# Block aggregates multiplied together with h, seven products for eight throughout, in a two-layer graph network

## The chip, the cores and the metric

The kernel runs on one core of one Trainium2 chip, in fp32. The metric is the device time of one launch in microseconds (us), the median of three runs. The profile is one profiled execution of the same program: its durations are exact for that execution, and its span (first to last instruction) is what the durations add up to.

## The reference

There are 64 graphs of 256 nodes and 512 features. Every graph passes through two layers. Both take `h = relu(layernorm(x))` and add their result to `x`. Cut to what matters:

```python
def layer0(x, adj, W):                      # W is 512 x 1024, [W1 | W2]
    h = relu(layernorm(x))
    T = adj / max(rowsum(adj), 1e-6)
    return x + relu(h @ W1.T + (T @ h) @ W2.T)

def layer1(X, A, Wv, bv, aw, ab, Wk, bk):   # Wk is 3 x 512 x 512
    h = relu(layernorm(X))
    Xw = h @ Wv + bv
    sj, si = Xw @ aw[:d, 0], Xw @ aw[d:, 0]
    e = leaky_relu(sj[:, None, :] + si[:, :, None] + ab, 0.2)
    a = A * exp(e)
    T = a / (rowsum(a) + 1e-12)
    return X + relu(h @ Wk[0] + T @ h @ Wk[1] + T @ T @ h @ Wk[2] + bk[0] + bk[1] + bk[2])
```

`T` is 256 x 256 for each graph. The scores need no 512 x 512 product, since `h @ Wv @ aw` is `h` times a vector that is worked out once.

## The kernel before

**Tiles.** 256 nodes are NC = 2 blocks of 128 partitions, 512 features are FC = 4 blocks. A product `h @ B` is cut into 2 x 2 blocks and computed as seven block products in place of eight (`seven`, L242; a Strassen form). `blocks` (L229) makes the four sums of blocks of the turned `h` on GpSimd; the sums of blocks of the weights are made once at the start (`combine`, L90). Each of the seven products is two matmuls, over two blocks of 128 of the features, into one of three PSUM banks, and ScalarE and VectorE move intermediate sums between them (L252 to L275).

**Turning.** TensorE wants its left operand with the summed index on the partitions, so `h`, adj and `T` are turned. `Flip` (L205) turns 32 x 32 squares on VectorE (L215), stores the four stripes to DRAM (L220) and loads them back in the turned order (L225). The first and last graphs are turned on TensorE (`flipped_on_pe`, L113).

**Layer 0** (`layer0`, L321): `seven` multiplies h by [W1 | W2] at once: 14 matmuls of 512 columns. Then `spread` (L278) adds `T (h W2)` in four ordinary matmuls of 512, and VectorE adds relu of the result to x (L332).

**Layer 1** is four pieces. `own` (L350) is `h Wk[0]` with the two score vectors as two extra columns per half: 14 matmuls of 258 columns. `transition` (L363) sends sj through DRAM to get it as a row on all partitions (ds, row), and makes T: exponentials on ScalarE (L377), maximum and products on VectorE (L380, L384), scaling (L393), turning. `pair` (L405) is `h [Wk[1] | Wk[2]]`: 14 matmuls of 512. `twice` (L410) adds `T q` (four matmuls of 512), copies `u` out (L425), and adds `T u` (four more); VectorE finishes and SP stores (L433, L435).

**Order.** Each piece is a generator that yields between steps, and strings of letters say which piece takes its next step: FIRST for the beginning, TURN for every graph from 4 on, LAST for the end. In one TURN the kernel works on layer 0 of graph g, own of g-1, pair and transition of g-2 and twice of g-3. Instructions stay in the order in which they are written, on each engine by itself. All DMAs are issued by SP.

The PSUM banks are three for layer 0 (bank0), three for layer 1 (bank1) and two that own shares with bank0 (bank2).

Of the kernel before, what the change touches and what calls it, by code (L numbers as in the profile page):

```python
# [15 lines left out]
P = 128  # L16
Q = 32
# [4 lines left out]


def bcast(ap, offset, n):

    return bass.AP(tensor=ap.tensor, offset=ap.offset + offset, ap=[[0, P], [1, n]])
# [3 lines left out]
def gnn_two_layers(ctx: ExitStack, tc: tile.TileContext, x, adj, w0, wv, bv, aw, ab, wk, bk, out):  # L30

# [7 lines left out]
    const = ctx.enter_context(tc.tile_pool(name="const", bufs=1))  # L56
    loads = ctx.enter_context(tc.tile_pool(name="loads", bufs=3))
    early = ctx.enter_context(tc.tile_pool(name="early", bufs=2))
    small = ctx.enter_context(tc.tile_pool(name="small", bufs=4))
    work = ctx.enter_context(tc.tile_pool(name="work", bufs=1))  # L60
    psum = ctx.enter_context(tc.tile_pool(name="psum", bufs=1, space=bass.MemoryType.PSUM))
    banks0 = [psum.tile([P, F], FP, name=f"bank0_{i}") for i in range(3)]
    banks1 = [psum.tile([P, F], FP, name=f"bank1_{i}") for i in range(3)]
    banks2 = [psum.tile([P, F], FP, name=f"bank2_{i}") for i in range(2)]
    dram = ctx.enter_context(tc.tile_pool(name="dram", bufs=2, space=bass.MemoryType.DRAM))

    X, A = {}, {}

    def load(g, what):
        if what is X:  # L70
            X[g] = loads.tile([P, NC, F], FP, name="x")
            nc.sync.dma_start(X[g], x[g].rearrange("(c p) f -> p c f", p=P))
        else:
            A[g] = loads.tile([P, NC, N], FP, name="a", bufs=4)
            nc.sync.dma_start(A[g], adj[g].rearrange("(c p) j -> p c j", p=P))

    names = ("b11", "b21", "b22", "t1", "t2", "t3", "t4")

    def forms(name, width):

        return {k: const.tile([P, FC // 2, width], FP, name=f"{name}_{k}") for k in names}

    B0, B1, B2 = forms("l0", F), forms("l1", F), forms("l1s", HW)
    bk_sb = const.tile([P, F], FP, name="bk_sb")
    c0 = const.tile([P, 1], FP, name="c0")
    ident = const.tile([P, P], FP, name="ident")
    mhalf = const.tile([P, NC], FP, name="mhalf")
    zero = const.tile([P, F], BF, name="zero")

    def combine(b, b12, eng=(nc.vector,) * 4):  # L90

        for e, to, x, y in zip(eng, ("t3", "t1", "t2", "t4"), ("b22", None, "b22", "b21"), (None, "b11", "t1", "t2")):
            e.tensor_sub(b[to], b12 if x is None else b[x], b12 if y is None else b[y])  # L93
            yield

    def turned_on_pe(blocks, banks):

        for i in range(0, len(blocks), FC):
            pt = next(banks).rearrange("p (k n) -> p k n", k=FC)
            for k, block in enumerate(blocks[i : i + FC]):  # L100
                nc.tensor.transpose(pt[:, k, :], block, ident)  # L101
            yield pt

    def weights_l0(w0_sb, b12, banks):

        for side, to in enumerate(((B0["b11"], B0["b21"]), (b12, B0["b22"]))):
            pts = turned_on_pe([w0_sb[oc][:, (side * FC + k) * P :][:, :P] for oc in range(FC) for k in range(FC)], banks)
            for oc, pt in enumerate(pts):
                for kh in range(2):
                    (nc.scalar.copy if oc % 2 else nc.vector.tensor_copy)(to[kh][:, :, oc * P : (oc + 1) * P],  # L110
                                                                         pt[:, 2 * kh : 2 * kh + 2, :])

    def flipped_on_pe(src, width, banks, pool, name, bufs=1):  # L113

        t = pool.tile([P, width // P, P, NC], FP, name=name, bufs=bufs)
        for c in range(NC):
            for pt in turned_on_pe([src[:, c, k * P : (k + 1) * P] for k in range(width // P)], banks):
                (nc.scalar.copy if c else nc.vector.tensor_copy)(t[:, :, :, c], pt[:, : width // P, :])
        return t

    def spare(name, bufs=1):

        return work.tile([P, 2, F], FP, name=name, bufs=bufs).rearrange("p s f -> p (s f)")

    def weights_l1():


        aw_sb = spare("x1", 4).rearrange("p (s f) -> p s f", s=2)
        wv_sb = [work.tile([P, NC, 2, HW], FP, name="e", bufs=2).rearrange("p c s w -> p (c s w)")[:, : 2 * F]
                 .rearrange("p (c f) -> p c f", c=2) for _ in range(2)]  # L130
        b12s = spare("u")[:, : FC // 2 * HW].rearrange("p (c w) -> p c w", w=HW)
        b12 = spare("o").rearrange("p (c f) -> p c f", f=F)
        scr, bv_sb = (work.tile([P, F], FP, name=n) for n in ("z0", "z1"))
        two = work.tile([P, FC, P, NC], FP, name="h1t", bufs=2).rearrange("p k n c -> p (k n c)")
        biases = [two[:, :F], two[:, F:], work.tile([P, F], FP, name="tt")]
        vc = small.tile([P, 2, FC], FP, name="vc", bufs=1)
        cc = small.tile([P, 2], FP, name="cc", bufs=1)
        ab_sb = small.tile([P, 1], FP, name="ab_sb", bufs=1)
        src = [wk[k].rearrange("(h c p) o -> h p c o", p=P, h=2) for k in range(NW)]
        nc.sync.dma_start(aw_sb, bcast(aw, 0, 2 * F))  # L140
        for h in range(2):
            nc.sync.dma_start(wv_sb[h], wv.rearrange("(h c p) o -> h p c o", p=P, h=2)[h])
        halves = ((b12s, 0, 1), (B2["b22"], 1, 1), (B2["b11"], 0, 0), (B2["b21"], 1, 0))
        for to, kh, col in halves:
            nc.sync.dma_start(to[:, :, :half], src[0][kh][:, :, col * half : (col + 1) * half])
            nc.gpsimd.memset(to[:, :, half + 1], 0.0)
        yield
        for to, k, kh in ((b12, 2, 0), (B1["b22"], 2, 1), (B1["b11"], 1, 0), (B1["b21"], 1, 1)):
            nc.sync.dma_start(to, src[k][kh])
        nc.sync.dma_start(bv_sb, bcast(bv, 0, F))  # L150
        nc.sync.dma_start(ab_sb, bcast(ab, 0, 1))
        for k in range(NW):
            nc.sync.dma_start(biases[k], bcast(bk, k * F, F))
        yield
        sums = combine(B1, b12, (nc.gpsimd,) * 4)
        for c in range(FC):
            next(sums)
            for s in range(2):
                nc.vector.scalar_tensor_tensor(scr, wv_sb[c // 2][:, c % 2, :], 1.0, aw_sb[:, s, :], op0=ALU.mult,  # L159
                                               op1=ALU.mult, accum_out=vc[:, s, c : c + 1])  # L160
            yield
        for to, kh, col in halves:
            nc.vector.tensor_copy(to[:, :, half], vc[:, col, 2 * kh : 2 * kh + 2])
        yield from combine(B2, b12s)
        for s in range(2):
            nc.vector.scalar_tensor_tensor(scr, bv_sb, 1.0, aw_sb[:, s, :], op0=ALU.mult, op1=ALU.mult,
                                           accum_out=cc[:, s : s + 1])
        nc.vector.scalar_tensor_tensor(c0, cc[:, 0:1], cc[:, 1:2], ab_sb, op0=ALU.add, op1=ALU.add)
        nc.vector.tensor_add(bk_sb, biases[0], biases[1])
        nc.vector.tensor_add(bk_sb, bk_sb, biases[2])  # L170
        yield


    def finished(steps):

        while True:
            try:
                next(steps)
            except StopIteration as end:
                return end.value  # L180

    def norm_relu(src):

        stats = small.tile([P, NC, 6], FP, name="stats")
        mv = small.tile([P, NC, 2], FP, name="mv")
        for c in range(NC):
            nc.vector.bn_stats(stats[:, c, :], src[:, c, :])  # L187
            nc.vector.bn_aggr(mv[:, c, :], stats[:, c, :])  # L188
            if c == 0:
                yield  # L190
        ve = small.tile([P, NC], FP, name="ve")
        nc.gpsimd.tensor_scalar(ve, mv[:, :, 1], LN_EPS, None, op0=ALU.add)  # L192
        rstd = small.tile([P, NC], FP, name="rstd")
        nc.gpsimd.tensor_tensor(rstd, ve, mhalf, op=ALU.pow)  # L194
        yield
        nmr = small.tile([P, NC], FP, name="nmr")
        nc.vector.scalar_tensor_tensor(nmr, mv[:, :, 0], -1.0, rstd, op0=ALU.mult, op1=ALU.mult)  # L197
        h = early.tile([P, NC, F], FP, name="h", bufs=1)
        for c in range(NC):
            nc.scalar.activation(h[:, c, :], src[:, c, :], AF.Relu, bias=nmr[:, c : c + 1],  # L200
                                 scale=rstd[:, c : c + 1])
            yield
# [345 lines left out]
```

## Time and profile before

| what | us |
|---|---|
| median of three runs (2642.81 to 2645.36) | 2644.55 |
| span of the profiled execution | 2643.6 |
| TensorE busy, share of the span | 2612.3, 99% |
| VectorE busy | 1204.4, 46% |
| ScalarE busy | 897.2, 34% |
| GpSimd busy | 524.2, 20% |
| granted TensorE clock, mean | 0.997 |

The profile lists, for each engine, groups of like instructions: source line, engine, operation, names of what is written and read, shape and count, then the busy time, the mean of one in ns, and the idle time ahead of them with what ended it. PE is TensorE, PEld its weight loads, DVE VectorE, ACT ScalarE, POOL GpSimd, SP the engine that issues DMAs. Matmul durations hold the time until the last result has left the array; the next matmul starts earlier, so the distance from start to start is the cost of one. An fp32 matmul appears as two records. In the timeline a line has start, length, engine, line, operation, names, shape and count. The chain of waits is followed back from the last instruction: each piece was released by the one before it.

### The profile page before, as it was taken

To read this page: it belongs to the slowest core of one execution; us is meant where nothing else is said; L and a number is where in the kernel's file an instruction comes from. 1 tells how busy PE (TensorE), PEld (TensorE's weight loads), DVE (VectorE), ACT (ScalarE), POOL (GpSimd) and SP (SyncE) were. 2 spreads that over 40 slices of the span, in tenths; PEclk is the share of its full clock that TensorE was granted. 3 is DMA by queue.
4 is the path that set the end of the run, shared out by engine and by line. 5 is a ranking of instruction groups with operands and counts; after the bars stand their busy time and mean duration, and the time that the engine had idled before them with its cause. 6 is when DMAs were issued, how large, how long until landed. Compare 5 with 4: busy or idle time off the path is not lost.

```text
span 2643.6 us, 23486 instructions
## 1 busy us (share of the span) xinstructions
PE 2612.3 (99%) x6983; PEld 1347.6 (51%) x6983; DVE 1204.4 (46%) x2664; ACT 897.2 (34%) x1807; POOL 524.2 (20%) x785
## 2 busy tenths in 40 slices
PE   7999999999999999999999999999999999999999
PEld 3544555555545545555555455555555554555554
DVE  5544444444444444444444444444444444444433
ACT  2333333333333333333333333333333333333332
POOL 3311211221121112111211221121112112211210
PEclk9999999999999999999999999999999999999999
DMA  5444454454454444444444445444445454454421
GB/s 183 108 126 119 108 118 110 111 123 106 120 120 100 121 115 112 116 111 112 123 103 123 116 103 122 113 112 116 111 114 123 100 125 116 104 122 109 110 74 44
DMA packets 576222, 298.93 MB, mean 113 GB/s; under 512 B 418784, under 2 KB 540640, under 8 KB 576096
## 3 DMA queue, kind: packets, MB, share of 16 engines
q1 hardware_dynamic: 576096, 297.44, 46.3%
q8 instruction: 56, 0.92, 0.1%
q14 instruction: 70, 0.57, 0.1%
HBM read 165.15 MB, written 132.19 MB: 112 GB/s over the span
## 4 chain that ended last, share of the span: by engine, by line
PE 97%; DVE 1%; issue 0%; ACT 0%; DMA 0%; SPq 0%; POOL 0%; DVEq 0%; ACTq 0%
PE bank L240 97%; PE bank L101 0%; DVE z L159 0%; DVE l_t L93 0%; DMA x<-in_x_dram 0%; DMA row<-ds 0%; DVE turned L215 0%; SPq L220 0%; DVE stats L187 0%; ACT z L377 0%; DVE nmr L197 0%; DVE o L433 0%; ACT an L296 0%; DVE l1s_t L93 0%; POOL rstd L194 0%
## 5 line engine op out<-in xcount | busy, mean ns | idle before, releaser
L240 PE MATMUL bank<-l_t,h1t_s 128*128 128x512 f32 x780 | 367.4, 594 | 0.7 <-ACT bank L252 0.7
L240 PE MATMUL bank<-l_t,h0t_s 128*128 128x512 f32 x756 | 356.9, 595 | 4.1 <-DVE l_t L93 3.4
L252 ACT COPY bank<-bank 128x512 f32<-128x512 f32 (+1 forms) x192 | 95.9, 499 | 710.7 <-PE bank L240 710.7
L215 DVE STREAM_TRANSPOSE turned<-h 128x512 f32<-128x512 f32 x252 | 178.4, 709 | 298.0 <-ACT h L200 298.0
L233 POOL TENSOR_TENSOR h0t_s<-h0t 128x256 f32<-128x256 f32 x63 | 53.3, 847 | 982.9 <-DMA h0t<-dh0t 880.3
L240 PE MATMUL bank<-l_b,h1t 128*128 128x512 f32 x520 | 244.4, 592 | 0.1
L240 PE MATMUL bank<-u,tt 128*128 128x512 f32 x512 | 242.1, 596 | 2.3 <-ACT u L425 2.3
L240 PE MATMUL bank<-q,tt 128*128 128x512 f32 x512 | 240.0, 592 | 1.3 <-DMA tt<-dtt 1.3
L240 PE MATMUL bank<-q,ant 128*128 128x512 f32 x512 | 232.5, 596 | 5.3 <-DVE q L275 5.3
L240 PEld LDWEIGHTS bank<-l_t,h0t_s 128*128 128x128 f32 x756 | 143.8, 191 | 183.5 <-issue 169.1
L240 PE MATMUL bank<-l_b,h0t 128*128 128x512 f32 x504 | 237.2, 593 | 0.0
L192 POOL TENSOR_SCALAR ve<-mv 128x2 f32<-128x2 f32 x128 | 29.2, 228 | 1020.4 <-DVE mv L188 1011.8
L200 ACT ACTIVATE h<-x,nmr,rstd 128x512 f32<-128x512 f32 x256 | 202.2, 818 | 17.7 <-DVE nmr L197 17.7
L240 PEld LDWEIGHTS bank<-l_t,h1t_s 128*128 128x128 f32 x780 | 147.7, 190 | 109.7 <-issue 97.0
L240 PEld LDWEIGHTS bank<-l1s_t,h1t_s 128*128 128x128 f32 x768 | 146.5, 191 | 102.7 <-issue 84.1
L240 PE MATMUL bank<-l1s_t,h1t_s 128*128 128x258 f32 x768 | 198.7, 381 | 0.0
L268 DVE TENSOR_TENSOR q<-bank,m 128x512 f32<-128x512 f32 x128 | 88.5, 692 | 202.2 <-PE bank L240 201.2
L332 DVE SCALAR_TENSOR_TENSOR x<-bank,x 128x512 f32<-128x512 f32 x128 | 88.5, 692 | 197.7 <-PE bank L240 197.7
L187 DVE BATCH_NORM_STATS2 stats<-x 128x6 f32<-128x512 f32 x256 | 172.2, 673 | 5.0 <-DMA x<-in_x_dram 5.0
L240 PEld LDWEIGHTS bank<-q,ant 128*128 128x128 f32 x512 | 100.8, 197 | 124.3 <-issue 109.4
L240 PEld LDWEIGHTS bank<-u,tt 128*128 128x128 f32 x512 | 100.6, 197 | 121.5 <-issue 88.4
L240 PEld LDWEIGHTS bank<-q,tt 128*128 128x128 f32 x512 | 100.5, 196 | 120.8 <-issue 116.3
(109 smaller groups left out, 3250.7 us busy)
## 6 DMA issues: line engine op xcount, KB each, us to landing
x<-in_x_dram SPq DMA_DIRECT2D x64, 512.0 KB, 5.6
dh1t<-turned SPq DMA_DIRECT2D x256, 128.0 KB, 2.8
h1t<-dh1t SPq DMA_DIRECT2D x64, 512.0 KB, 3.9
out_dram<-o SPq DMA_DIRECT2D x64, 512.0 KB, 3.2
dh0t<-turned SPq DMA_DIRECT2D x248, 128.0 KB, 2.9
h0t<-dh0t SPq DMA_DIRECT2D x62, 512.0 KB, 4.2
a<-in_adj_dram SPq DMA_DIRECT2D x64, 256.0 KB, 3.2
dant<-turned SPq DMA_DIRECT2D x248, 64.0 KB, 1.9
```

The lines of the kernel that those rows point to most:

```text
L187: nc.vector.bn_stats(stats[:, c, :], src[:, c, :])
L192: nc.gpsimd.tensor_scalar(ve, mv[:, :, 1], LN_EPS, None, op0=ALU.add)
L200: nc.scalar.activation(h[:, c, :], src[:, c, :], AF.Relu, bias=nmr[:, c : c + 1], scale=rstd[:, c : c + 1])
L215: nc.vector.transpose(self.turned.rearrange("p b r c -> p c b r")[:, c], src.rearrange("p c (b s) -> p c b s", s=Q)[:, c])
L233: nc.gpsimd.tensor_add(s1, a21, a22)
L240: nc.tensor.matmul(ps, lhs, rhs, start=start, stop=stop, skip_group_check=True)
L252: nc.scalar.copy(r, p)
L268: nc.vector.tensor_add(c22, p, m167)
L332: nc.vector.scalar_tensor_tensor(x1[:, c, :], banks[1 + c], 0.0, x[:, c, :], op0=ALU.max, op1=ALU.add)
```

## The change

The kernel is rewritten around three ideas.

1. Aggregation comes first. Layer 0 computes `z = T h` and then `[h | z] @ [W1 ; W2]` as one block product with the long inner dimension: each of the seven products sums over h and z in one bank before it is decoded (`main`). Layer 1 computes `z = T h`, `q = z Wk[2]`, and then `h Wk[0] + z Wk[1] + T q`, again as seven products over all three terms (`outer`). `T T h Wk[2]` is thus `T (z Wk[2])`, and the aggregate stays in its encoded form: `spread` writes the four blocks of z and the three sums of them that the next product wants as left operands.
2. Every product is a seven-product form, those with T too. `left_of_t` makes the four sums of blocks of T, `right_of_h` those of h, both on GpSimd. `spread` takes h as the stationary operand and T as the moving one, 128 columns wide, so that z comes out turned. The scores are four products with accumulation on VectorE of h with two vectors `v = Wv @ aw`, made at the start and spread through DRAM.
3. The order is data. `Plan.add` records each instruction with what it reads and writes; `emit` sorts each engine's instructions by a number from a table (AT), one per instruction of a stage, plus graph x TURN, plus a shift for the first and last five graphs (SHIFT).

In the steady turn TensorE works on aggregate and layer0 of graph g, `once` (layer 1's z) and `inner` (q) of g-1, and `outer` of g-2. One DMA per piece and the ways of turning stay as they were.

```diff
+EDGE = 5
+TURN = 41.62
+AT = {
+    "aggregate": (-3.8, 0.1, -3.6, 5.6, -18.4, -16.1, 2.2, -2.0, 2.2, 3.7, 9.3, 4.8, 4.4, 4.5, 5.0, 5.2, 14.3, 6.9, 13.8, 12.7, 10.0, 17.0, 11.4,
+        18.9, 21.4),
...
+class Plan:
+    def stage(self, name, graph=None, shift=None):
+        self.name, self.graph, self.count = name, graph, 0
+        self.base = 0.0 if graph is None else graph * self.turn + self.shift.get((name, shift), 0.0)
+    def emit(self):
+        queues = {}
+        for i in sorted(range(len(self.ops)), key=lambda i: self.ops[i][3]):
+            queues.setdefault(self.ops[i][0], []).append(i)
...
+    def left_of_t(tt, s):
+        (t, tk), (sv, sk) = tt, s
+        a11, a12, a21, a22 = (t[:, k, :, c] for c in range(2) for k in range(2))
+        tks, ks = [tk, tk + "'"], parts(sk, 4)
+        pool_op("tensor_add", 0.55, sv[:, 0], a21, a22, tks, ks[0])
+        pool_op("tensor_sub", 0.55, sv[:, 1], sv[:, 0], a11, tks + ks[:1], ks[1])
+        pool_op("tensor_sub", 0.5, sv[:, 2], a11, a21, tks, ks[2])
+        pool_op("tensor_sub", 0.5, sv[:, 3], a12, sv[:, 1], tks + ks[1:2], ks[3])
...
+    def spread(left, right, out, banks):
+        (z, zk), (m, mk), (bx, by) = out, MZ[0], banks
+        def turned(k, b, cols, start=False):
+            (l, lk), (r, rk) = left[k], right[k]
+            def run():
+                for i in range(2):
+                    at = cols.start + i * P
+                    matmul(bank[b][:, at : at + P], r[:, i * P : (i + 1) * P], l, start and i == 0)
+            add("PE", 0.001684 * half, run, lk + rk, [f"bank{b}"])
+        turned(1, by, lo, True)
+        turned(5, bx, lo, True)
+        copy(*m1, by, lo)
+        minus(*m15, *m1, bx, lo)
+        turned(2, by, lo)
+        turned(6, by, hi)
+        turned(4, bx, lo)
+        turned(7, bx, hi)
+        copy(*zf(0), by, lo)
+        plus(*u, by, hi, *m15)
+        copy(*zf(3), bx, lo)
+        plus(*zf(2), bx, hi, *u)
+        turned(3, by, hi)
+        plus(*zf(1), by, hi, *m15)
+        pool_op("tensor_sub", 0.85, z[:, 4], z[:, 3], z[:, 0], at(3)[1] + at(0)[1], f"{zk}.4")
+        pool_op("tensor_add", 0.85, z[:, 5], z[:, 4], z[:, 2], at(4)[1] + at(2)[1], f"{zk}.5")
+        pool_op("tensor_add", 0.85, z[:, 6], z[:, 4], z[:, 1], at(4)[1] + at(1)[1], f"{zk}.6")
...
+    def main(terms, banks, bias):
+        p, r, d = banks
+        step(5, p, lo, terms, True)
+        if bias:
+            l5, k5 = lo5, "lo5"
+            minus(l5[:, 1], ["lo5.1"], bk_hi, ["bk"], p, lo)
+        else:
+            copy(m5_0, ["m5_0"], p, lo)
+        step(1, p, lo, terms, True)
...
+        step(6, p, lo, terms)
...
+        step(7, p, lo, terms)
...
+        step(2, r, lo, terms)
+        step(3, r, hi, terms)
+        step(4, d, lo, terms)
...
+    def turn1(g):
+        norm_relu(g, of(X, g), next(norms), (h, hk))
+        for s in range(2):
+            for c in range(NC):
+                add("DVE", 0.85, lambda s=s, c=c: nc.vector.scalar_tensor_tensor(scr.rearrange("p c n -> p (c n)"), h[:, c, :], 1.0, v_sb[:, s, :],
+                                                                               op0=ALU.mult, op1=ALU.mult, accum_out=sj[:, s, c : c + 1]),
+                    [f"{hk}.{c}", "v"], parts(sck) + [f"{sjk}.{s}{c}"], port=True)
...
+    def once(g):
+        zs[g] = spread(lefts[g], right_of_h(rights1.pop(g), HF[1]), ZG[0], (6, 7))
+    def inner(g):
+        step(1, by, lo, terms, True)
+        step(7, bx, lo, terms, True)
+        copy(*m1, by, lo)
+        plus(*m17, bx, lo, *m1)
+        step(2, by, lo, terms)
+        step(6, by, hi, terms)
+        step(3, bx, lo, terms)
+        step(4, bx, hi, terms)
+        copy(*b11, by, lo)
+        plus(*u3, by, hi, *m17)
+        copy(*t3, bx, lo)
+        plus(*t2, bx, lo, *b11)
+        plus(*b21, bx, hi, *u3)
+        step(5, by, hi, terms)
+        plus(*b22, by, hi, *m17)
+        pool_op("tensor_sub", 0.85, nt1[0], t2[0], b22[0], t2[1] + b22[1], nt1[1][0])
+        pool_op("tensor_sub", 0.85, t4[0], b21[0], t2[0], b21[1] + t2[1], t4[1][0])
+    def outer(g):
+        banks = (3, 4, 5)
+        main([(left_of_h(H1T[0], S1[0]), weights(W1F, "l1", 0)), (zs.pop(g), weights(W1F, "l1", 1)), (lefts.pop(g), qs.pop(g))], banks, True)
+        finish(g, banks)
...
+    ORDER = ("aggregate", "prepare", "layer0", "prepared", "turn1", "loads", "moved", "once", "inner", "turned1", "outer", "transition")
-    TURN = "EU NL NEU mUIL NL NNU NEL ENU EUL ENL ENL EP NL L IO MP MO MP O MP EMO NMP O P O O MOP"
```

In the turn of the changed kernel the names are: `s0` and `s1` the sums of blocks of the turned h for layer 0 and 1 (the text also says s00 and s10 for their buffers), `hf0` and `hf1` those of h as right operand, `sa` and `st` those of T, `ag` and `zg` the seven forms of z, `qf` those of q, `ant` and `tt` the turned T, banks 0 to 2 layer 0, 3 to 5 outer, 6 and 7 the spreads and inner. `step(k)` is one of the seven products over all its terms.

## The prediction

> **What bounds the kernel now.** I read the page's first part (busy time of each engine), then its chain of waits, then the timeline of TensorE over one round of the loop.
>
> ```profile
> PE 2612.3 (99%) x6983; PEld 1347.6 (51%) x6983; DVE 1204.4 (46%) x2664; ACT 897.2 (34%) x1807; POOL 524.2 (20%) x785
> ...
> 149.00 2448.84 PE bank L240 x6540
> ...
> 1300.21 1.88 PE L240 MATMUL bank<-u,tt 128*128 128x512 f32 x4
> 1301.93 1.88 PE L240 MATMUL bank<-l_t,h0t_s 128*128 128x512 f32 x4
> ...
> 1315.66 1.03 PE L240 MATMUL bank<-l1s_b,h1t 128*128 128x258 f32 x4
> 1316.54 1.88 PE L240 MATMUL bank<-l_t,h1t_s 128*128 128x512 f32 x4
> ...
> 1340.65 1.88 PE L240 MATMUL bank<-u,tt 128*128 128x512 f32 x4
> ...
> 2603.14 0.60 PE L101 MATMUL bank<-ident,an 128*128 128x128 f32 x4
> 2603.58 1.88 PE L240 MATMUL bank<-l_t,h1t_s 128*128 128x512 f32 x4
> ```
>
> TensorE is the bound, and it does not wait: from 149.00 to 2597.84 us the chain is one piece of L240. So the time is TensorE's instructions times their spacing, and everything on the other engines is cover. The starts give the spacing. Every fp32 matmul is two records ("passes"). Four of 512 columns take 1301.93 - 1300.21 = 1.72 us, 0.429 each; four of 258 take 0.88, 0.218 each; four transposes of 128 columns, each with a weight load of its own, 0.44, 0.110 each. That is a straight line: two cycles of 2.4 GHz per column and some 2.5 ns. The mean durations of the groups (594 and 381 ns) hold the drain and aren't the spacing.
>
> Check on a whole turn: 40 matmuls of 512 and 14 of 258 are 80 x 0.429 + 28 x 0.2177 = 40.42 us. The timeline has u,tt at 1300.21 and again at 1340.65: 40.44. So 64 turns are 2587, and 56 of the span's 2643.6 us are filling and draining (for 0 to 149 and 2597 to the end TensorE's work is spread thin). The median of the runs, 2644.55, lies 1 us above the span; I add that at the end.
>
> The helpers' prices come from the groups by line and shape, and the DMA issues (last number: us to landing):
>
> ```profile
> L187 DVE BATCH_NORM_STATS2 stats<-x 128x6 f32<-128x512 f32 x256 | 172.2, 673 | 5.0 <-DMA x<-in_x_dram 5.0
> L268 DVE TENSOR_TENSOR e<-bank,m_s 128x258 f32<-128x258 f32 x64 | 27.3, 426 | 14.4 <-PE bank L240 14.4
> L159 DVE SCALAR_TENSOR_TENSOR z<-e,x 128x512 f32<-128x512 f32 x8 | 10.4, 1306 | 0.1
> L166 DVE SCALAR_TENSOR_TENSOR z<-z,x 128x512 f32<-128x512 f32 x2 | 1.4, 686 | 0.0
> L265 ACT COPY m_s<-bank 128x258 f32<-128x258 f32 x64 | 24.0, 375 | 20.8 <-PE bank L240 20.7
> L234 POOL TENSOR_TENSOR h1t_s<-h1t_s,h1t 128x256 f32<-128x256 f32 x65 | 74.3, 1143 | 5.1
> L234 POOL TENSOR_TENSOR h0t_s<-h0t_s,h0t 128x256 f32<-128x256 f32 x63 | 46.7, 742 | 4.9
> L235 POOL TENSOR_TENSOR h1t_s<-h1t 128x256 f32<-128x256 f32 x65 | 39.7, 611 | 0.0
> ant<-dant SPq DMA_DIRECT2D x62, 256.0 KB, 3.0
> row<-ds SPq DMA_DIRECT2D x64, 128.0 KB, 4.6
> ds<-sj SPq DMA_DIRECT2D x64, 1.0 KB, 3.2
> ```
>
> **What the Trainium skill says.** "TensorE: Matmul & The Clock Gate", Back-to-back issue gap: a warm matmul follows the last one after N/2.4 + 2.5 ns; the trace agrees for 512, 258 and 128 columns if N is doubled. The same page, LDWEIGHTS: a load costs its columns over 1.2, so 107 ns for 128, and is drawn ahead of running matmuls; the transposes at 110 ns agree, the records of PEld (190 to 197 ns) don't say so by themselves. "FP8 and Floating Point Precision", TensorE Precision Notes: true fp32 is four passes, here two records of two. "GPSIMD Engine Reference", Key points: GpSimd shares its SBUF interfaces with VectorE and suffers under vector instructions with two SBUF inputs; the trace agrees, L159 taking 1306 ns beside GpSimd's weight sums against 686 for its like at L166, and L234 1143 ns for h1t_s against 742 for h0t_s.
>
> **The change, part by part.** *TensorE per graph.* Removed: own's 14 matmuls of 258, pair's 14 and layer0's 14 of 512, twelve aggregating ones of 512 (q,ant; q,tt; u,tt). Added: two spreads of 7 products x 2 matmuls of 128 columns (28), main of layer 0 with 7 x 4 of 256 (28), inner 7 x 2 (14), outer 7 x 5 (35). So 154 passes of 256 at 0.216 = 33.26, and 56 of 128 at 0.110 = 6.16: 39.4 us against 40.42. A gain of 1.0 us a turn, 64 in all, is all there is to win, if TensorE stays as dense as now.
>
> *Weight loads* double, from 108 to 210 a turn. Hidden behind 256 columns as they are behind 258. Behind 128 columns the trace has only transposes: lower bound nothing; upper bound the whole PEld record, 56 x (0.19 - 0.11) = 4.5 us a turn. I take nothing, since 110 ns was seen with a new weight each time.
>
> *VectorE.* Gone: seeds 1.4, evacuations of pair and own (1.4 + 0.85), layer0's evacuations 1.4, si and sj 0.55. Added: scores as four products of h1 with v (0.69 at L166 to 1.3 at L159 each: 2.8 to 5.2), 15 additions and subtractions of 256 columns out of PSUM (0.43 by the 258 form of L268: 6.5) and outer's 0.7. Sum of the turn, from the rows: 26 to 28 us of 39.4, against 18.8. *ScalarE*: 17 copies of 512 or 258 columns become 12 of 256 (0.37): 12 us against 14. *GpSimd*: 24 additions of 128x256 (0.61 to 0.85 in the rows of L233 to L236, mean 0.74, 1.14 under contention), 8 of 128x128 (estimate from half of these: 0.4 to 0.55), four small ones 1.9: 23 us, at worst 34, against 8.2. *SP* issues 25 DMAs a turn before and after, of the same sizes. No engine but TensorE is full.
>
> *Waits.* TensorE's order in the built program interleaves four graphs, and I laid each wait against the TensorE work between producer and consumer, origin at aggregate's first product. Evacuations that TensorE waits for have 0.25 us or more to spare (step 6 of layer 0 follows its copy by 0.25; inner's second step by 0.2). Three places are tight:
> - VectorE before the next aggregate. Inner's last product ends at 38.0; in VectorE's queue stand b21, a 0.67 bn_stats and then b22 (0.43), which frees bank 7: about 39.2 to 39.5, wanted at 39.4. Cost 0 to 0.3 us a turn.
> - SP's queue: the scores are done at 27.6 to 28.7; ds lands 3.2 later; row, queued behind, waits for it, and ant's load for the next graph stands behind row on SP: issued at 31.4 to 32.5, landed 3.0 later. GpSimd waits for ant, and queued behind that are hf0 and outer's s10, 2.4 us in all: 36.8 to 37.9, wanted by TensorE at 37.6. Cost 0 to 0.3, up to 1.2 if GpSimd's four run at contended speed.
> - max, the two products with A and tot on VectorE, 3.7 to 5.7, before lo5 (TensorE wants it at 8.2): contended they end at 7.8. Cost nothing.
>
> I take 0.2 us a turn, 13 in all; ends 0 and 0.65 for the likely case.
>
> *Filling.* All of layer 1 now needs z, so TensorE's order is aggregate and layer 0 of graphs 0 and 1, then once(0). Weights arrive first and adj of graph 0 as the twelfth load; layer0(0) ends at some 38 us (before, its second spread was at 43.70). From there finish, statistics, two relus, two score products, ds 3.2, row 4.6, four exponentials 2.1, max and products 1.9, transpose, four stores 3.4, load 2.8 and GpSimd's sums make 29, crowded 32, against 15 us of graph 1's work: once(0) at 70. Once and inner of graph 0 have no other work between their steps: 9 us and some 7 of waits. At 86 us one turn's work is done. Bounds 75 and 110.
>
> *Draining.* The order has 31 us of work between layer0(63) and once(63), enough for the chain without its DMA flip (tt by TensorE). Then once, inner and outer of the last two graphs run with gaps of some 0.8 us at each evacuation: 17 us, and 5 for the last evacuation and store (it is 4.5 now). Bounds 14 and 35.
>
> *Sum.* 86 + 63 x (39.4 + 0.2) + 22 = 2603 us of span, and 1: **2604 us**, 1.5% less.
>
> **Rivals.**
> 1. *The helpers' queues stall TensorE* (slower). Place: GpSimd's queue behind ant, where s10, hf0 and sa wait, and VectorE's before bank 7. Price: each us of stall a turn is 63. From 0.84 us a turn the gain is gone (86 + 63 x 40.24 + 22 + 1 = 2644). At 2 us, which GpSimd reaches if most of its additions run at 1.14, it gives 2717. For it: GpSimd's work triples, VectorE's rises by half, each wait is in-order. Against it: GpSimd at worst is 34 of 39.4, and the stretches where it matters are short.
> 2. *Weight loads bind the 128-column passes*: 4.5 us a turn more, 2888 us. For it: PEld records of 190 ns. Against it: transposes at 110.
> 3. *Filling and draining eat the gain*, with 30 us more than I count, or a stall near 0.8: about 2640. For it: the chain of graph 0 bare of cover. Against it: it occurs once.
> 4. That TensorE computes less is sure from the order; no rival there.
>
> **How the numbers follow.** Likeliest case 0.68: stall 0 to 0.65, filling within its bounds, own range 2575 to 2632. Case 3: 0.09. Case 1: 0.17. Case 2: 0.06. No change is within 0.2%, 2639 to 2650. Faster: 0.68 and part of case 3, 0.72; same 0.05; slower 0.23. The range for 8 in 10 goes from 2575 to 2680, into case 1.
>
> **What would show it.** In the changed profile: TensorE's own spacing (0.216, 0.110) in the timeline; a turn of 39.4 to 39.9 from aggregate to aggregate; once(0) near 70; idle before `ant`-fed and `h1t_s`-fed groups naming POOL, before bank 7 naming DVE. A spacing of 0.19 at 128 columns, or a turn over 40.2, would make it wrong.

## The result and the profile after

| | us |
|---|---|
| before, median of eight runs (2642.28 to 2645.36) | 2643.45 |
| after, median of eight runs (2635.4 to 2638.87) | 2636.35 |
| ratio after / before, 95% interval | 0.9974 [0.9964, 0.9984] |
| span of the profiled execution after | 2634.6 |

The change makes the kernel faster by 7 us. The forecast was 2604, so 32 us of the expected gain of 40 are missing. First the page's busy times, then TensorE's busy share and the granted clock, both in tenths, in forty slices of the span:

```profile
PE 2572.8 (98%) x13520; PEld 2309.4 (88%) x13520; DVE 1498.9 (57%) x3686; ACT 696.2 (26%) x1680; POOL 1463.5 (56%) x2317
...
PE   5799999999999999999999999999999999999998
...
PEclk8799999999999999999999999999999999999999
```

TensorE is still the bound, with 39.5 us less busy time than before (2612.3). Its gaps sit at the left end: in the first two slices (66 us each) it is busy for some 0.5 and 0.7 of the time, and the granted clock is 0.8 and 0.7. The chain of waits shows where (start, length, what):

```profile
7.16 8.38 DMA qf<-in_L_gnn_Wk_dram
15.56 6.37 DMA qf<-in_L_gnn_Wk_dram
21.95 6.38 DMA lq<-in_L_gnn_Wk_dram
30.57 0.80 ACT an L407 x2
32.35 4.51 PE bank L296 x24
...
46.94 8.56 DMA dv<-vc
55.90 6.85 DMA a<-in_adj_dram
...
89.16 4.96 DVE z L471 x4
...
120.32 36.91 PE bank L296 x192
...
239.66 2140.04 PE bank L296 x11324
```

Up to 63 us the longest pieces of the chain are loads of layer 1's weights, the store of the vectors v (`dv`) and the load of graph 3's adjacency. None of these is an operation on graph 0, whose scores take up v from 70 us on. At 89 us stands graph 0's transition. From 120 us on the chain is TensorE. Its timeline gives the marks by which the prediction was built:

```profile
30.62 1.12 PE L246 MATMUL bank<-ident,an 128*128 128x128 f32 x4 [8.21 <-ACT h0t L252]
...
61.59 0.61 PE L296 MATMUL bank<-ant,h1n 128*128 128x128 f32 x4
...
70.83 1.22 PE L296 MATMUL bank<-ant,h1n 128*128 128x128 f32 x4 [8.17 <-ACT mz L308]
...
102.71 1.22 PE L296 MATMUL bank<-tt,h1n 128*128 128x128 f32 x4 [3.53 <-DMA tt<-dtt]
...
112.19 5.45 PE L296 MATMUL bank<-lq,zg 128*128 128x256 f32 x24 [0.28 <-POOL zg L259]
117.47 1.03 PE L296 MATMUL bank<-l,s 128*128 128x256 f32 x4
...
223.38 0.62 PE L296 MATMUL bank<-tt,hf 128*128 128x128 f32 x4
...
2486.25 0.62 PE L296 MATMUL bank<-tt,hf 128*128 128x128 f32 x4
```

layer0(0) ends at 61.6, once(0) starts at 102.7 and inner(0) ends at 117.5. By then TensorE has done two aggregates, two layer0, one once and one inner: one turn's work (the second aggregate and layer0 take as long as an outer, 15.2 us against 15.1 by the spacings), the "86" of the prediction. The group `tt,hf` comes once a turn: (2486.25 - 223.38) / 57 = 39.70 us. So the span splits into 117.5 of filling + 63 x 39.70 + 16.0 of draining (what is left of 2634.6). The end of the filling and the turn are what the versions below are compared by.

### The profile page after: what moved, and what is told of

It is laid out like the page before. It is cut to its first block, busy times and chain, and to the rows that moved or that the text cites. A ratio compares the mean times of both kernels' runs of the same rounds, so it can differ in the third digit from the quotient of the medians.

```text
span 2634.6 us, 39436 instructions
## 1 busy us (share of the span) xinstructions
PE 2572.8 (98%) x13520; PEld 2309.4 (88%) x13520; DVE 1498.9 (57%) x3686; ACT 696.2 (26%) x1680; POOL 1463.5 (56%) x2317
## 4 chain that ended last, share of the span: by engine, by line
PE 95%; DMA 2%; DVE 2%; ACT 1%; issue 1%; POOL 0%; SPq 0%; DVEq 0%; ACTq 0%; POOLq 0%
PE bank L296 95%; DMA qf<-in_L_gnn_Wk_dram 1%; DMA dv<-vc 0%; DMA a<-in_adj_dram 0%; DVE z L471 0%; DMA lq<-in_L_gnn_Wk_dram 0%; ACT an L407 0%; DMA x<-in_L_gnn_W_dram 0%; DVE qf L311 0%; DVE z L607 0%; DMA dan<-turneda 0%; DVE stats L208 0%; ACT qf L308 0%; DVE x L398 0%; ACT si L453 0%
## 5 line engine op out<-in xcount | busy, mean ns | idle before, releaser
L296 PE MATMUL bank<-l,s 128*128 128x256 f32 x2048 | 527.6, 380 | 3.3 <-DVE bank L311 2.3
L296 PE MATMUL bank<-l,zg 128*128 128x256 f32 x1792 | 459.6, 379 | 0.0
L296 PE MATMUL bank<-l,ag 128*128 128x256 f32 x1792 | 451.9, 380 | 2.3 <-ACT ag L308 2.3
L296 PEld LDWEIGHTS bank<-l,s 128*128 128x128 f32 x2048 | 380.1, 191 | 51.1 <-issue 2.6
L296 PE MATMUL bank<-lq,zg 128*128 128x256 f32 x1792 | 399.0, 379 | 2.5 <-DVE zg L311 1.4
L296 PEld LDWEIGHTS bank<-lq,zg 128*128 128x128 f32 x1792 | 339.7, 190 | 51.2 <-DVE zg L311 2.5
L296 PEld LDWEIGHTS bank<-l,ag 128*128 128x128 f32 x1792 | 341.6, 191 | 48.9 <-ACT ag L308 2.8
L296 PEld LDWEIGHTS bank<-l,zg 128*128 128x128 f32 x1792 | 330.5, 189 | 39.5
L296 PE MATMUL bank<-l,h1t 128*128 128x256 f32 x780 | 202.2, 382 | 5.2 <-ACT bank L308 3.3
L296 PE MATMUL bank<-l,h0t 128*128 128x256 f32 x756 | 194.7, 380 | 1.1 <-DVE bank L383 0.6
```

The costliest lines, as they stand in the source:

```text
L296: nc.tensor.matmul(ps, lhs, rhs, start=start, stop=True, skip_group_check=True)
```

## The experiments

**Where is the loss: once, or in each turn?** Both kernels with half the graphs.

```diff
     G, N, F = x.shape
+    G = 32
```

> The changed kernel with graphs 32 to 63 left out (their outputs are not written). Its time against the full one splits the total into a cost per graph and a cost paid once. Theory A (the loss is paid once, in the filling): 32 graphs are 32 x 39.68 = 1270 us, so 2636 - 1270 = 1366 us, and some 96 us of it are paid once. Theory B (each turn stalls, the once-only cost is the 56 us of the kernel before): a turn is (2636 - 56) / 64 = 40.3, so 1346 us.

> The kernel before with graphs 32 to 63 left out. Both theories: a turn of 40.44, so 2643 - 32 x 40.44 = 1349 us, 56 of it paid once. Under theory A the order of the two kernels turns over at this size: the kernel before is 17 us faster than the changed one with 32 graphs. Under theory B the changed one stays some 3 us ahead.

Measured: 1366.9 us for the changed kernel (1365.8 to 1368.3) and 1348.0 for the kernel before (1346.7 to 1350.2), as Theory A had them. A turn costs (2636.35 - 1366.88) / 32 = 39.67 us after and (2643.34 - 1347.96) / 32 = 40.48 before; paid once are 2636.4 - 64 x 39.67 = 97 us and 2643.3 - 64 x 40.48 = 53. Theory B is out. Each turn wins 0.81 us, and filling and draining give 45 back, so the two kernels meet at 45 / 0.81, some 55 graphs. With 32 the change is a loss of 19 us.

**The first block: VectorE's queue.** VectorE's timeline of the changed kernel, ahead of aggregate(0):

```profile
21.21 0.89 DVE L607 SCALAR_TENSOR_TENSOR z<-l,h1n 128x512 f32<-128x512 f32 x1 [1.88 <-DMA l<-in_L_gnn_Wv_dram]
...
28.36 0.69 DVE L624 TENSOR_TENSOR lq<-qf,lq 128x512 f32<-128x512 f32 x1 [6.24 <-DMA lq<-in_L_gnn_Wk_dram]
28.96 0.22 DVE L405 RECIPROCAL deg<-deg 128x2 f32<-128x2 f32 x2
```

A weight difference (L624), of which TensorE has no need before graph 0's inner product at 110.8 us, waits 6.24 us for its load. The reciprocal of graph 0's degrees, whose input was ready at 18 us, waits behind it. The edit is the place of this one instruction in the table:

```diff
-        -238.5, 28.7, 43.7, -3.3,
+        28.0, 28.7, 43.7, -3.3,
```

> One product of the weights of the second layer (the difference that makes lq_5, on VectorE) goes behind the reciprocals of the degrees in VectorE's queue; nothing else changes. Theory A (in the filling, in-order queues are blocked by weights that come late): TensorE's wait of 8.2 us before the transposes of an falls to some 2 us, aggregate(0) starts near 26 instead of 32.4, and 3 to 6 us of the total go, 2630 to 2633 us. Rival B (the chain of graph 0 through loads, scores and row is what sets the filling, whatever starts earlier): within 2 us of 2636.

Measured: 2629.8 us (2629.5 to 2629.9), ratio to before 0.9948 [0.9935, 0.996], so 6.6 less than the change, a little more than Theory A's 3 to 6. Rival B is out for this wait. TensorE's timeline of this version:

```profile
25.91 1.19 PE L296 MATMUL bank<-ant,h0n 128*128 128x128 f32 x4 [0.18 <-ACT lq L621]
...
111.46 1.03 PE L296 MATMUL bank<-l,s 128*128 128x256 f32 x4
```

aggregate(0) starts at 25.9 instead of 32.4, the filling ends at 111.5 instead of 117.5, and the turn stays at 39.70.

**Three blocks together.** SP's queue of the changed kernel:

```profile
24.07 0.37 SPq L597 DMA_DIRECT2D l<-in_L_gnn_Wk_dram  x1
46.94 0.37 SPq L610 DMA_DIRECT2D dv<-vc  x1
55.51 0.34 SPq L612 DMA_DIRECT2D v_sb<-dv  x1
55.90 0.43 SPq L197 DMA_DIRECT2D a<-in_adj_dram  x1
56.42 0.42 SPq L194 DMA_DIRECT2D x<-in_x_dram  x1
```

SP issues nothing for 23 us: it waits for the eight products of Wv with aw (L607), the last of which ends on VectorE at 46.9, then 8.6 us for `dv` to land. Behind these stands adj of graph 3, and VectorE's row sum of it (L403, at 62.8) stands ahead of the residual and the statistics of graph 0, and these ahead of the relu behind which ScalarE's copy `mz` waits. That is the 8.17 us before 70.83 above. The edit takes in the one of the first test (lq_5), and moves the six late products and graph 3's loads:

```diff
-        ..., -293.2, -203.1, -159.6, -81.9, -54.5, -36.5, -27.6, -3.8, ...
+        ..., -293.2, -203.1, -202.9, -159.6, -145.0, -144.0, -143.0, -142.0, ...
-        -238.5, 28.7, 43.7, ...
+        28.0, 28.7, 43.7, ...
-    3: {... "loads": -38.0, ...
+    3: {... "loads": -90.0, ...
```

> Three blocks of the filling are taken away together, by places in the queues alone: lq_5 behind the reciprocals on VectorE; the six late products of Wv with aw ahead of aggregate(0) on VectorE, so that dv is stored at some 28 us instead of 47; adj and x of graph 3 ahead of dv on SP's queue. Theory A: waits of 8.2 - 2, 3.2 and 8.2 us before 71 us go, aggregate(2) starts at 100 to 106 us instead of 118, total 2618 to 2624 us. Rival B (layer 1 of graph 0 is bare of cover by its own length): once(0) stays near 102, total within 3 us of 2636. Rival C (TensorE's cold clock in the filling, 0.76 to 0.83 granted, is the loss): the gaps close but the passes stay slow, 5 us at most are won, 2631 or more.

Measured: 2624.75 us (2624.1 to 2625.9), 0.993 [0.9917, 0.9942]: 11.6 less than the change. TensorE's timeline of this version:

```profile
26.87 1.20 PE L296 MATMUL bank<-ant,h0n 128*128 128x128 f32 x4 [0.22 <-DVE ant L252]
...
58.25 1.22 PE L296 MATMUL bank<-ant,h1n 128*128 128x128 f32 x4 [5.77 <-ACT mz L308]
...
85.30 1.14 PE L296 MATMUL bank<-l,h1t 128*128 128x256 f32 x4 [3.34 <-ACT bank L308]
...
91.79 1.22 PE L296 MATMUL bank<-tt,h1n 128*128 128x128 f32 x4 [4.49 <-DMA tt<-dtt]
```

once(0) moves from 102.7 to 91.8, the filling ends at 105.6, so Theory A's mechanism holds and rival B is out. The total is a microsecond above A's range, and well below the 2631 of rival C: the last of the three waits shrank from 8.2 to 5.8 only, since the copy `mz` still stood behind the relu of graph 0 in ScalarE's queue, and this relu behind graph 0's statistics.

**Is it the half-speed TensorE?** After the long waits (8.17 us before 70.83, 3.53 before 102.71) groups of four 128-column passes take 0.85 us from start to start instead of 0.44. The Trainium skill, "TensorE: Matmul & The Clock Gate", What's actually happening, says that the clock is 1.2 GHz after an idle window of about 3.4 us and goes to 2.4 after as long a busy one. The passes here agree in their rate, half as fast; no run here measures the windows. Summed over the changed kernel's filling from 20 us on (start to start, less the full-speed spacing, waits left out) it is 14 to 18 us, the more if the passes just ahead of a wait are counted. To take it away, idle transposes run in the waits:

```diff
+    "warm": (-392.0, -240.0, -148.0, 60.5),
...
+        for n, b in ((5, 0), (6, 0), (6, 0), (38, 3)):
+            def run(n=n, b=b):
+                for _ in range(n):
+                    nc.tensor.transpose(bank[b][:, :P], ident, ident)
+            add("PE", 0.11 * n, run, ["ident"], [f"bank{b}"])
```

> The version with the three blocks taken away (2625 us) and, besides, 55 transposes of the identity matrix on TensorE in its waits of the filling (5 and 12 of them between 17 and 24 us, 38 just ahead of once(0)), into banks that are cleared before they are used. They compute nothing. Theory C (in the filling TensorE runs at half speed after each wait until it has been busy for some us: groups of four 128-column products at 0.85 us instead of 0.44): aggregate(0), layer0(0) and once(0) then start at full speed, 4 to 8 us go, 2617 to 2621 us. Theory A (waits alone): no gain, within 1.5 us of 2625, or more if the transposes are in the way.

Measured: 2628.5 us (2627.7 to 2629.0), 0.9944 [0.9932, 0.9957], 3.8 worse than without them. The edit was at fault: the last group stood behind the second product of once(0), not ahead of the first, and held TensorE for 6.3 us. Put right, with 26 at place 56.3:

> The version with idle transposes again, its last group put right: 26 transposes of the identity ahead of the first product of once(0) instead of 38 behind its second, where they stood in the way (6.3 us of them on the path). Theory C (half speed after a wait is a cost of its own): once(0) and inner(0) of graph 0 take 11 to 12.5 us instead of 14.0 from the first product to inner's end, and with 1 us before it in aggregate(0) and layer0(0) the total is 2621 to 2623 us against 2625 for the version without them. Theory A (waits alone): within 1 us of 2625.

Measured: 2624.0 us (2623.3 to 2627.7), 0.9933 [0.9919, 0.9947], 0.8 less than without transposes, within the spread, and so on Theory A's side. Its timeline of TensorE (line numbers are one higher here and in the versions that keep the transposes):

```profile
26.70 1.19 PE L297 MATMUL bank<-ant,h0n 128*128 128x128 f32 x4 [0.18 <-DVE ant L253]
27.68 1.06 PE L297 MATMUL bank<-sa,hf 128*128 128x128 f32 x4
...
86.49 3.59 PE L663 MATMUL bank<-ident 128*128 128x128 f32 x26
89.98 0.72 PE L297 MATMUL bank<-tt,h1n 128*128 128x128 f32 x4
91.18 0.71 PE L297 MATMUL bank<-st,hf 128*128 128x128 f32 x4 [0.47 <-POOL st L260]
93.07 0.72 PE L297 MATMUL bank<-tt,h1n 128*128 128x128 f32 x4 [1.18 <-ACT mz L309]
```

once(0) runs at full speed, and waits for GpSimd's sum and ScalarE's copy take the place of most of its slow passes: once and inner took 13.3 us against 13.8, where Theory C asked for 11 to 12.5. Here the slow clock hides behind the waits. The test reaches no further than once(0), though: aggregate(0) still starts at half speed (0.98 us to the next group), as in the version without transposes, and graph 1's aggregate does too. By the same count 11 to 14 us of slow passes are left, against 13 to 17 without the transposes. The filling ends at 103.3 us instead of 105.6; in the profiled executions the draining took 1.4 us of this back, though no edit touched it. What the slow clock costs in the rest of the filling is not shown.

**The chain of graph 0 first.** In the changed kernel the two products of the transition (L471, in the chain at 89.16) took 2.45 and 2.55 us while GpSimd summed weights (L536):

```profile
88.53 2.79 POOL L536 TENSOR_TENSOR l<-l,qf 128x1024 f32<-128x1024 f32 x1
89.16 2.45 DVE L471 SCALAR_TENSOR_TENSOR z<-z,a 128x256 f32<-128x256 f32 x1
91.41 2.40 POOL L536 TENSOR_TENSOR l<-l,l 128x1024 f32<-128x1024 f32 x1
...
91.55 2.55 DVE L471 SCALAR_TENSOR_TENSOR z<-z,a 128x256 f32<-128x256 f32 x1
```

```diff
-    "turn1": (..., 41.4, 46.7, 50.6, 44.2, ...
+    "turn1": (..., 41.4, 46.1, 46.2, 44.2, ...
-        ..., -38.2, 50.4, 51.5, 103.2, 18.1, -112.2,
-        28.0, 28.7, 43.7, ...
+        ..., -38.2, 55.5, 56.0, 103.2, 18.1, -112.2,
+        40.0, 40.5, 43.7, ...
-    0: {... "transition": -3.1, ...
+    0: {... "transition": -8.0, ...
```

> The version with the three blocks taken away and, besides, the chain of graph 0 from its scores to tt put first in the queues: the second si activation next to the first, the whole transition of graph 0 4.9 us earlier in every queue, lq_5 and lq_6 behind the scores on VectorE, two weight sums of the second layer on GpSimd behind the transition (beside them a product of 128x256 on VectorE took 2.46 us instead of 0.42). Theory A (that chain, with what stands in its way, sets once(0)): once(0) starts at some 83 us instead of 92, total 2615 to 2618 us. Rival B (its length is its DMAs alone): once(0) not before 89, total 2622 or more.

Measured: 2621.45 us (2620.7 to 2622.1), 0.9917 [0.9903, 0.993], 3.3 less than with three blocks away; 7 to 10 were expected. The price of contention is plain in VectorE's timeline of this version, where GpSimd's two sums come later:

```profile
74.37 0.38 DVE L471 SCALAR_TENSOR_TENSOR z<-z,a 128x256 f32<-128x256 f32 x1
```

But once(0) starts at 89.0, not 83, and the result lies next to rival B's 89 and 2622. On VectorE aggregate(1)'s last sums stood behind a transpose for graph 3 that waited 3.8 us for a store; ScalarE's copies of these sums stood ahead of graph 0's exponentials; and the stores of tt now share SP's queue with those of h. Moving aggregate(1) ahead didn't help:

```diff
-    1: {"aggregate": -13.8, ...
+    1: {"aggregate": -20.0, ...
```

> The last version with all of aggregate(1) 6.2 us earlier in the queues as well, so that its copies don't stand behind the relu of graph 0's second layer (TensorE waited 5.8 us there). Theory A: if TensorE's own work of graph 1 ends later than graph 0's chain, this brings 1 to 4 us more, 2612 to 2616 us. Rival: the chain of graph 0 alone sets once(0), and aggregate(1)'s work stands in its way on VectorE: 0 to 2 us worse than the last version.

Measured: 2622.2 us (2621.7 to 2623.5), 0.9921 [0.9908, 0.9935]; once(0) at 86.1, inner(0)'s end at 102.9 against 103.2, nothing in the total. The total is the rival's, but not for its reason: once(0) did start 3 us earlier, and waits inside it took that back (its second `tt,h1n` group started at 91.2, against 91.5).

**The wait in each turn.** ScalarE's timeline of the changed kernel in mid-run:

```profile
1309.83 0.37 ACT L308 COPY qf<-bank 128x256 f32<-128x256 f32 x1 [2.77 <-DVE qf L311]
1310.10 0.48 ACT L453 ACTIVATE si<-sj,c 128x2 f32<-128x2 f32 x2
1310.48 0.36 ACT L308 COPY mz<-bank 128x256 f32<-128x256 f32 x1
```

Two activations of 128x2, whose readers stand behind the copy in the same queue, stand ahead of this copy, for which TensorE waits.

```diff
-    "aggregate": (..., 2.2, 3.7, 9.3, 4.8, ...
+    "aggregate": (..., 2.2, 3.7, 5.0, 4.8, ...
```

> The changed kernel with one place moved: the copy of m1 (mz) of the aggregate goes ahead of the two small si activations in ScalarE's queue. In the steady turn TensorE's aggregate waits some 0.1 us for that copy (0.56 us to the next group instead of 0.44). Theory A: the wait goes, 0.1 us a turn, 60 turns, 6 us: 2630 us, and a turn of 39.58 instead of 39.68. Rival: the copy waits for its product anyway, the turn stays at 39.68 and the total within 2 us of 2636.

Measured, on the changed kernel alone: 2630.0 us (2628.1 to 2630.6), 0.9948 [0.9936, 0.9961], 6.4 less. The turn is 39.58, so Theory A holds, and the order in ScalarE's timeline is the one meant:

```profile
1306.85 0.37 ACT L308 COPY qf<-bank 128x256 f32<-128x256 f32 x1 [2.77 <-DVE qf L311]
1307.12 0.38 ACT L308 COPY mz<-bank 128x256 f32<-128x256 f32 x1
1307.38 0.49 ACT L453 ACTIVATE si<-sj,c 128x2 f32<-128x2 f32 x2
```

**Both together.** The chain of graph 0 first, and the copy at 5.0:

> The filling with the chain of graph 0 put first (2621.5 us) and the copy of m1 ahead of the si activations as in the single test (6.4 us less than the changed kernel). If the two are independent, one paid once and one in each turn: 2615 us, 2614 to 2617. If the si activations, which stand together now, already gave that: 2620 or more.

Measured: 2620.6 us (2620.1 to 2621.4), 0.9915 [0.9902, 0.9928]; the turn is 39.69. The miss has its cause in the edits: with both si at 46.1 and 46.2 they stood ahead of the copy (41.6 + 5.0 = 46.6) again. Next, with the idle transposes and graph 3's preparation later:

```diff
-    3: {... "prepare": -6.7, ...
+    3: {... "prepare": -2.0, ...
```

> Everything together: the last version, the idle transposes in their right place, and the preparation of graph 3 4.7 us later in the queues, because its transpose on VectorE waited 3.8 us for a store ahead of aggregate(1)'s last sums. Theory A with C: 2 to 3 us from the transposes and 1 to 3 us from that wait: 2609 to 2613 us. Rival: the DMAs of graph 0 alone are left as the bound before once(0), and nothing more than 1 us goes: 2614 or more.

Measured: 2618.0 us (2616.9 to 2621.5), 0.9906 [0.9892, 0.992], 2.6 less than without these two edits and 5 above Theory A's range; the filling ends at 99.2 instead of 102.6, the turn is still 39.69. The two edits were not tried apart, but the trace shows graph 3's at work: the transpose's wait is gone from VectorE's queue, graph 0's exponentials start at 67.4 instead of 71.4 and the load of tt is issued at 81.7 instead of 85.6. Then the copy ahead of the si activations again, and once(0) earlier:

```diff
-    "aggregate": (..., 2.2, 3.7, 5.0, 4.8, ...
+    "aggregate": (..., 2.2, 3.7, 4.0, 4.8, ...
-    0: {... "once": -5.1, ...
+    0: {... "once": -8.0, ...
```

> The last version with the copy of m1 put ahead of the si activations again (they had been moved together to a place ahead of it, and the turn had stayed at 39.69), and once(0) 2.9 us earlier in the queues, so that its copy doesn't stand behind the relu of graph 1 (TensorE waited 1.7 us there). Theory A: the turn goes to 39.58, as where the copy was moved alone, 6 to 7 us, and 1 us in the filling: 2610 to 2612 us. Rival (with the filling shortened, the copy is no longer what ends the wait): a turn of 39.68, 2617 us.

Measured: 2617.4 us (2614.8 to 2619.5), 0.9903 [0.9887, 0.992], where 2610 to 2612 were expected. The turn is 39.58, as Theory A had it, but the filling ends at 102.3. Without the shift of once(0):

> The last version without its shift of once(0): the copy of m1 ahead of the si activations in every turn, the filling as in the version before it (inner(0) ended there at 99.2 us; with the shift at 102.3). Theory A (the shift of once(0) itself cost 3 us, since an aggregate sum waits on VectorE behind it, and the turn's gain is independent): a turn of 39.58, inner(0) ends at 99 to 100 us, profiled span 2608 to 2610, median 2610 to 2614 us. Rival (the copy's new place in the first turns costs the 3 us): inner(0) ends at 102 again and the span stays at 2612.

Measured: 2611.0 us (2609.0 to 2612.7), 0.9876 [0.986, 0.9893]. Its marks on TensorE are the start of aggregate(0), the end of layer0(0), the start of once(0) and the end of inner(0):

```profile
26.80 1.19 PE L297 MATMUL bank<-ant,h0n 128*128 128x128 f32 x4 [0.18 <-DVE ant L253]
...
51.00 0.62 PE L297 MATMUL bank<-ant,h1n 128*128 128x128 f32 x4
...
84.12 0.62 PE L297 MATMUL bank<-tt,h1n 128*128 128x128 f32 x4
...
99.59 1.03 PE L297 MATMUL bank<-l,s 128*128 128x256 f32 x4
```

The filling ends at 99.6, the turn is 39.58: the two kinds of loss are independent, and the shift had cost the 3 us (by the trace of that version three score products of graph 1, which waited for a relu behind the copy, stood in VectorE's queue ahead of once(0)'s last sums). This version is 1.2% faster than before and 25 us faster than the change. Beyond the idle transposes it differs from the changed kernel only in places in queues.

## Why the prediction was wrong

| term of the sum | predicted | after | last version |
|---|---|---|---|
| filling, until a turn's work is done | 86 | 117.5 | 99.6 |
| turn | 39.6 | 39.70 | 39.58 |
| draining | 22 | 16.0 | 16.5 |
| sum: first and third, and 63 turns | 2603 | 2634.6 | 2609.8 |

*The step that failed is the filling*: 31.5 us too short and above its own bound of 110. By its parts: layer0(0) was to end at 38 and ended at 61.6 (23.6 late); from there once(0) was to take 32 and took 41.1 (9 late); once and inner of graph 0 were to take 16 and took 14.8. The prediction counted when loads arrive and how long graph 0's operations last. For the filling it did not ask which instruction stands ahead of them in each in-order queue. The runs show what stood there, by how much earlier the filling ended without it: a weight difference waiting for its load (6.0 us by itself), the products for v with `dv` and graph 3's loads behind them (5.9 more), and weight sums, graph 0's chain and graph 3's transpose (6.0 more, with the idle transposes). So 17.9 of the 31.5 us went. Places in the queues alone had brought 14.9 of them; the rest came with the step in which graph 3's preparation and the idle transposes were put in together.

The other 13.6 stay in the last version, ahead of layer0(0)'s end: it is at 51.0, still 13 after the 38. From there on the prediction's terms come out: 33.1 us to once(0) against 32, and 15.5 for once and inner against 16. Dense, aggregate(0) and layer0(0) would take 15.2 us (28 passes at 0.110 and 56 at 0.216), so an end at 38 leaves a start at 22.8. By the trace they start at 26.8 and take 24.2: aggregate(0) begins at half speed, waits for evacuations, and has graph 1's transposes between itself and layer0(0), which waits some 0.55 us at each of three evacuations. The prediction had put no number to these. That is read from the trace and was not tried apart, so the cause of these 13 us stays open between the late start, the waits and the slow clock. The range of the filling was too narrow as well: a chain of thirty operations through five queues that no row of the profile before had shown was given -11 and +24 us.

*The turn was right.* 154 x 0.216 + 56 x 0.110 = 39.4; measured 39.70. The stall of 0.2 (0 to 0.65) measured 0.3, worth 6 us of the error, which the draining below gave back by luck. Its place was not among the three named: VectorE, SP and GpSimd were watched, and ScalarE's queue, dismissed with "0.25 us or more to spare", held 0.12 of it.

*The helpers.* GpSimd 1136 us in 2000 (22.6 a turn) against 23; ScalarE 10.7 against 12; VectorE 22.9 against 26 to 28. That sum was added up wrongly: the terms listed with it (18.8, less 5.6 for what goes, and 2.8 to 5.2, 6.5 and 0.7 for what comes) give 23.2 to 25.6. A score product took 0.74 us on average, near the lower of the two rows used. The upper one, 1306 ns "beside GpSimd's weight sums", was misread: it is the mean of eight products of 0.64 to 2.75 us, of which the two longest (2.75 and 2.71) came after the start of a GpSimd sum of 128x1024, and the four shortest took 0.64 to 0.68. The timeline of the kernel before:

```profile
56.71 0.65 DVE L159 SCALAR_TENSOR_TENSOR z<-e,x 128x512 f32<-128x512 f32 x1
57.25 2.35 POOL L93 TENSOR_TENSOR l_t<-l_b,o 128x1024 f32<-128x1024 f32 x1
...
57.40 2.75 DVE L159 SCALAR_TENSOR_TENSOR z<-e,x 128x512 f32<-128x512 f32 x1
```

So the price of that contention, some four times, was in the profile before. Rival 1, helpers that stall TensorE beyond 0.84 us a turn, didn't come.

*Weight loads* are hidden, as taken: in steady work four 128-column passes take 0.44 to 0.47 us from start to start (aggregate's, once's), although each has a weight load whose record lasts 190 ns. Rival 2 is out.

*Rival 3* (filling and draining eat the gain, about 2640) is what happened, at a chance of 0.09. Its argument against, "it occurs once", was no argument: against 0.8 us a turn, once is 55 turns.

*The draining* was over-sized by 6 us, with the mechanism right: the gaps at the evacuations were 0.4 to 0.6 us where 0.8 were taken, and the last evacuation and store took 4.8 against 5.

## What to carry to other kernels

When a change wins a little in each round of a loop, write the time as once + rounds x turn and measure two sizes: the point where the two kernels meet tells whether the gain is real at your size. In the filling of a software pipeline look, for each first-needed instruction, at what stands ahead of it in its own queue and what that waits for; work for later (weights, next inputs) goes behind the work of the first round, or far enough ahead that its load has landed. Moving an instruction of a shared stage to help the first round also moves it in every other one, so check the steady order again.

## What the runs showed of the hardware

- A store of 4 KB (`dv<-vc`) took 8.56 us to land, and 8.5 to 9.8 in five other versions; `ds<-sj` of 1 KB takes 3.2 as a median.
- A VectorE product of 128x256 with two operands in SBUF took 2.45 and 2.55 us beside a GpSimd sum of 128x1024, and 0.38 and 0.42 without it. By the trace both ended 0.3 us after the sum beside them (89.16 + 2.45 against 88.53 + 2.79, and 91.55 + 2.55 against 91.41 + 2.40), so their length is what was left of the sum, and less than their own length on top. In the kernel before a product of 128x512 took 2.75 us beside such a sum, and its like just ahead 0.65.
- Idle transposes ahead of once(0) brought its passes to full speed (0.44 to 0.56 us for four, against 0.85), and once and inner from 13.8 to 13.3 us: waits on GpSimd and ScalarE came in the place of the rest.
- After a wait of 1.7 us ahead of once(0)'s second `tt,h1n` group the passes went at half speed in one execution (the last version: 1.02 us to the next start) and at full speed in another (the version two before it: 0.56), with the end of inner(0) within 0.4 us.
